# A four-stream graph-attention stack on one core: a clamp moved to ScalarE, new start times and pauses of the streams, and new transfer prices in its planner

## The chip, the core and the metric

The kernel runs on one core of a Trainium2 chip. The metric is device time in microseconds (us). The kernel before takes 2759.6 us, the median of 3 runs (2759.0 to 2762.83).

## The reference, cut to what matters

`x` is 32 batches of 512 nodes by 256 features, `adj` one 512 x 512 adjacency matrix for all. Each batch goes through four graph-attention layers, each one on the relu of a layer norm, with a residual:

```python
h = maximum(layernorm(x), 0); x = x + L0(h)      # attention, masked by adj, elu
h = maximum(layernorm(x), 0); x = x + L1(h)      # attention, masked by adj, relu
h = maximum(layernorm(x), 0); x = x + L2(h)      # the same with 4 heads of 64, elu
h = maximum(layernorm(x), 0); x = x + L3(h)
# L3: out = relu(x @ mlp1_w + b)                  (256 -> 512)
#     out = elu(_gat(out, no mask, W_fc)) + out   and _gat ends in an elu itself
#     out = relu(out @ mlp2_w + b)                (512 -> 256)
#     out = relu(elu(_gat(out, adj, W_hand)) + out)
```

So layer 3 holds two elus of an elu. With q = exp(v), the inner elu is max(v, 0) + min(q, 1) - 1, and the outer one on top adds exp(min(q, 1) - 1) - 1 on the negative side. All arithmetic is float32.

## The kernel before, in words

**Work.** A batch of 512 nodes is four tiles of 128 rows. A layer norms its rows (VectorE statistics at L653 and L654, ScalarE Ln and Exp for the root at L656 and L657, VectorE subtraction at L660 or L664), transposes them on TensorE (L442) and takes the relu on the way out of PSUM into `hT` (L674), multiplies by the weights (`values`, L434) into `v`, and builds the attention weights `w` (L737, one VectorE instruction for 128 x 512). For L737 a row of scores has to stand on all partitions: a short transpose, a copy on ScalarE (L749), a DMA of the row to DRAM (L751) and one that spreads it back over the 128 partitions (L757). The weighted sums run on TensorE (`averages`, L434), and VectorE takes the reciprocal of their denominator (L769). Layer 2 runs its four heads on quarters of the array (L438, "128*32"). Layer 3's unmasked attention is done by sorting in 31 of the 32 batches: rows are scattered to DRAM by an indirect DMA on GpSimd (L1025), prefix sums are made and written to a table (L1071), and the rows are gathered back (L1079). The last batch does it by plain sums (`attend`).

**The clamp.** `elu2_plus1` (L794 to L798) is called 194 times, 190 of them on 128 x 512: VectorE takes min(q, 1) (L796), ScalarE exp of that minus 1 (L797, the -1 is a bias column `minus1`), VectorE adds it to the relu part (L798).

**Four streams.** Batch b belongs to stream b mod 4; each stream is a Python generator that yields virtual times, and the loop over `ready` (L1190 to L1208) always runs the stream that is earliest. `after_us(u)` (L428) gives the virtual time of the next step: the step's begin, plus STRETCH times the TensorE time that it issued, plus SLOW times u. Stream i begins at i * LEAD + late. In its first batch a stream also waits PAUSES[3b + i] behind each of layers 0, 1 and 2. `setup`, which finishes the weights and the mask, is a fifth stream with its own spacing. All this only fixes the order in which the program is written.

**The planner.** The program is built twice. In the rehearsal `jobs_of` and `in_order` (L165 to L376) simulate it with a price for each instruction and let each engine take, of what is ready, what was written first; the order that results is then forced on each engine's queue (`arrange`). Two tiles of one buffer tag must open in the order in which they are written. So a stream that is written late can't open its first `xn` before the earlier-written streams have opened theirs, even where engines are idle. Transfers are priced in `price` (L110, its transfers from L126) by kind, from LANDING and SHORT; only loads of inputs also share a pipe of 350 bytes per ns (`job.flux`).

Of the kernel before, what the change touches and what calls it, by code (L numbers as in the profile page):

```python
# [67 lines left out]
class Job:  # L68
# [9 lines left out]
HANDOVER = {"PE": 40.0, "DVE": 33.0, "Activation": 33.0, "Pool": 70.0, "SP": 28.0}  # L78
LANDING = {
    "sums": 5600.0, "spread": 4300.0, "table": 6500.0, "x": 10000.0, "order": 4100.0, "g": 6800.0, "out": 4500.0,  # L80
    "adj": 9000.0,
}
SHORT = {"table": 5200.0, "row": 2600.0, "out": 4500.0}
SWITCH = 93.0
# [25 lines left out]
def price(job, outs, ins, in_psum):  # L110
# [15 lines left out]
    if op == "DMACopy":  # L126
        name, _, s = outs[0]
        kind = name.split("_")[0].rstrip("0123456789")
        large = elements(s) * s[0][1] > 5000
        job.took = LANDING.get(kind, 6000.0) if large else SHORT.get(kind, 3300.0)  # L130
        if kind == "spread":
            job.took += 900.0 * (ins[0][1] // 512)
        if ins[0][0].startswith("in_") and not (kind == "x" and ins[0][1] >= 4 * 512 * 256):
            job.took, job.flux = 2500.0, max(160.0, 4.0 * elements(s) * s[0][1] / 350.0)
        job.holds = (2000.0 if kind == "order" else 1290.0) if e == "Pool" else 600.0 if kind in ("sums", "table") else 400.0
        return
# [264 lines left out]
def fast(ctx, tc, plan, flag, x, adj, w0, a0, w1, a1, w2, a2, mlp1_w, mlp1_b, mlp2_w, mlp2_b,  # L401
# [9 lines left out]
    NS = 4  # L411
    LEAD = 81.69
    GO = 7.0
    PAUSES = (1.98, 20.79, 0, 9.87, 13.42, 5.98, 12.87, 2.43, 0, 28.8, 13.7, 0)
    SLOW = 1.53
    STRETCH = 1.75

# [35 lines left out]
    nc.vector.memset(eps, EPS)  # L453
    minus1 = const.tile([P, 1], FP, name="minus1")
    nc.vector.memset(minus1, -1.0)
    seen = const.tile([P, 5 * B], FP, name="seen")
# [219 lines left out]
    def turned(xn, when):  # L676

        hT = work.tile([P, KF, N], FP, tag="hT", name="hT", bufs=3)
        turn_pair(xn, hT, 0)
        yield when  # L680
        turn_pair(xn, hT, 2)
        yield after_us(0.26)
        return hT
# [8 lines left out]
    def values(hT, w, rs=None):  # L692

        v = work.tile([P, NT, F + 3], FP, tag="v", name="v", bufs=4)
        for t in range(NT):
            ps = bank()
            for k in range(KF):
                matmul(
                    ps[:, :F + 3], hT[:, k, t * P:(t + 1) * P], w[:, k, :], start=(k == 0), stop=(k == KF - 1)
                )  # L700
            pj = v[:, t, F:F + 1]
            if rs is None:
                nc.scalar.activation(v[:, t, F:], ps[:, F:F + 3], AF.Exp)
                nc.scalar.activation(v[:, t, :F], ps[:, :F], AF.Copy, scale=pj)
            else:
                nc.scalar.activation(v[:, t, F:], ps[:, F:F + 3], AF.Exp, scale=rs[:, t:t + 1])
                both = small([1], "both")
                nc.vector.tensor_tensor(both, rs[:, t:t + 1], pj, op=OP.mult)
                nc.scalar.activation(v[:, t, :F], ps[:, :F], AF.Copy, scale=both)
            if t + 1 < NT:  # L710
                yield after_us(0.32)
        yield after_us(0.7)
        return v

    def linear_t(inT, w, bias, name, bufs):
# [3 lines left out]
        for f in range(ft):  # L719
            p = bank()  # L720
            for k in range(kt):
                matmul(p, w[:, k, f * P:(f + 1) * P], inT[:, k, :], start=(k == 0), stop=(k == kt - 1))
            nc.scalar.activation(o[:, f, :], p, AF.Relu, bias=bias[:, f:f + 1])
            yield after_us(0.05 if f == ft - 1 else 2.73)
        return o
# [46 lines left out]
    def plain(hT, w, rs=None, far=False):  # L772
        v = yield from values(hT, w, rs)
        r = None
        if far:
            r = spread(rows_out(v[:, :, F + 2], 1)[0, :])
            yield after_us(11.34)
        wt = weights(lambda t: v[:, t, F + 2:F + 3], lambda j: v[:, j, F + 1:F + 2], r=r)
        note(v[:, :, F:])
        yield after_us(0.41)  # L780
        return v, wt
# [12 lines left out]
    def elu2_plus1(r, q):  # L794

        nc.vector.tensor_scalar(q, q, 1.0, None, op0=OP.min)  # L796
        nc.scalar.activation(q, q, AF.Exp, bias=minus1)  # L797
        nc.vector.tensor_tensor(r, q, r, op=OP.add)  # L798

    def layer0(xt, xn, rs, when):  # L800
        v, wt = yield from plain((yield from turned(xn, when)), W0, far=True)
        xn, rs = new_xn(), small([NT], "rs")
        for t0 in range(0, NT, 2):
            r, q = pair(), pair("q")
            for i in range(2):
# [3 lines left out]
                if i == 0:  # L809
                    yield after_us(0.56)  # L810
            add_elu(xt[:, t0:t0 + 2, :], r, q)
            norm(xt, xn, rs, t0, True)
            last, when = when, after_us(0.48)
            if t0 == 0:
                yield after_us(0)
        yield last
        return xn, rs, when

    def layer1(xt, xn, rs, when):
        v, wt = yield from plain((yield from turned(xn, when)), W1, rs, far=True)  # L820
        xn, rs = new_xn(), small([NT], "rs")
        for t0 in range(0, NT, 2):
            r = pair()
            for i in range(2):
                p, rd = averages(v, wt, t0 + i)
                nc.scalar.activation(r[:, i, :], p, AF.Relu, scale=rd)
                if i == 0:
                    yield after_us(3.06)
            xr = xt[:, t0:t0 + 2, :]
            nc.vector.tensor_tensor(xr, xr, r, op=OP.add)  # L830
            norm(xt, xn, rs, t0, True)
            last, when = when, after_us(1.98)
            if t0 == 0:
                yield after_us(0.04)
        yield last
        return xn, rs, when

    def layer2(xt, xn, rs, when):
        hT = yield from turned(xn, when)
        v = work.tile([P, NT, NH, CH], FP, tag="v", name="v2", bufs=4)  # L840
        for t in range(NT):
# [10 lines left out]
            )  # L852
            yield after_us(1.87 if t + 1 < NT else 0.3)
        row_d = rows_out(v[:, :, :, D + 2], NH)
# [3 lines left out]
        def begin():  # L858
# [3 lines left out]
            )  # L862
            return after_us(0.05)

# [5 lines left out]
        )  # L870
        yield after_us(14.86)
        begin()
        note(v.rearrange("p t h c -> p (t h) c")[:, :, D:])
        yield after_us(0.87)
        when = begin()
        for g, parts in enumerate(plan):
# [9 lines left out]
            nc.scalar.copy(s, p)  # L886
            yield after_us(1.08)
            if g < 2:
# [23 lines left out]
            if g:  # L912
# [3 lines left out]
                add_elu(xt[:, :, (g - 1) * 2 * D:g * 2 * D], y, q)  # L916
            yield after_us(3.1)
        xn, rs = new_xn(), small([NT], "rs")
        for t0 in range(0, NT, 2):
            norm(xt, xn, rs, t0, False)  # L920
        yield after_us(4.83)
        return xn, rs, after_us(1.14)

# [27 lines left out]
    def attend(oT, b):  # L951

        halves, ends = fc_values()
        for c in range(2):
            for t in range(NT):
                project_half(oT, halves, ends, c, t)
                yield after_us(0.48)
# [4 lines left out]
        yield after_us(0.73)  # L962
        ys = []
        for t in range(NT):
# [9 lines left out]
            ys.append(y)  # L974
            yield after_us(0.14)
            if t:
                mlp_in(oT, ys[t - 1], t - 1)
                yield after_us(0.1)
        yield after_us(0)
# [3 lines left out]
    def sort_attend(oT, b):  # L983
# [6 lines left out]
        for t in range(NT):  # L990
            project_half(oT, halves, ends, 0, t)
            yield after_us(1.43)
        project_half(oT, halves, ends, 1, 0)
        yield after_us(0.78)
# [3 lines left out]
        yield after_us(5.75)  # L998

# [8 lines left out]
        note(ends)  # L1008
        sort = after_us(3.88)
        yield after_us(0.32)  # L1010
        for t in range(1, NT):
            project_half(oT, halves, ends, 1, t)
            yield after_us(3.04)
        for t in range(NT):
# [6 lines left out]
        for c in range(2):  # L1021
# [17 lines left out]
            sort = after_us(0.46)  # L1039
        places = table[:N, :].rearrange("(p t) (k c n) -> p (t k) c n", t=NT, k=2, c=2)  # L1040
        sort = after_us(0.54)
        for c in range(2):
# [15 lines left out]
            yield after_us(1.92)  # L1058

# [12 lines left out]
            nc.sync.dma_start(table[N:, c * C:(c + 1) * C], tot[P - 1:, :])  # L1072
            sort = after_us(6.33)
        yield after_us(12.5)
        got, when, gs = [], [], []
# [10 lines left out]
        gather(1)  # L1086
        landed = after_us(9.82)
        for t in range(NT):
# [12 lines left out]
            got.append(y)  # L1101
            landed = after_us(0.46)
            when.append(after_us(12.63))
            if t == 0:
# [4 lines left out]
        mlp_in(oT, got[-1], NT - 1)  # L1109
        yield after_us(0.11)  # L1110

    def layer3(xt, xn, when, b):
# [6 lines left out]
        for t0 in range(0, NT, n):  # L1119
            y, q = pair()[:, :n, :], pair("q")[:, :n, :]  # L1120
            for i in range(n):
                p, rd = averages(v, wt, t0 + i)
                nc.scalar.activation(q[:, i, :], p, AF.Exp, scale=rd)
                nc.scalar.activation(y[:, i, :], p, AF.Relu, scale=rd)
                yield after_us(0)
            elu2_plus1(y, q)
# [39 lines left out]
    def batch(b):  # L1166
        if b < NS:
            first_norm(b)
            yield after_us(20.8)
        else:  # L1170
            yield after_us(0.8)
        xt, xn, rs = normed.pop(b)
        when = after_us(2.46)
        for i, layer in enumerate((layer0, layer1, layer2)):
            xn, rs, when = yield from layer(xt, xn, rs, when)
            if b < NS:
                yield after_us(PAUSES[3 * b + i])
        if b + NS < B:
            xts[b + NS] = load_x(b + NS)
# [9 lines left out]

    ready = {i: i * LEAD + late for i, late in enumerate((0, 4.35, 4.97, 5.59))}  # L1190
    streams = [stream(i) for i in range(NS)]
    early = setup()
    ready[NS] = 1.42
    while ready:
        i = min(ready, key=ready.get)
        if i == NS:
            turn[0] = NS - 1
            ready[i] += 19.61
            if next(early, early) is early:
# [463 lines left out]
```

## Time and profile before

| what | value |
|---|---|
| median of 3 runs | 2759.6 us |
| the profiled execution, its own time | 2780.08 us |
| its span, first to last instruction | 2778.3 us |
| granted TensorE clock, mean | 0.993 |
| PE busy | 2711.2 us, 98% |
| DVE (VectorE) busy | 2288.7 us, 82% |
| ACT (ScalarE) busy | 1625.7 us, 59% |
| POOL (GpSimd) busy | 515.4 us, 19% |
| chain that ended last | PE 69%, DVE 23%, ACT 5% |

Times in the profile are of one execution. Busy times of PE are modelled where matmuls overlap, so that an instruction's duration on PE is longer than the distance to the next. A wait is written as "who <- what it waited for"; idle time of an engine that isn't the bound costs nothing. Groups are told apart by line, engine, tile names and shape.

### The profile page before, as it was taken

The page shows a single profiled execution, that of the slowest core. Times are in us where ns is not written, and L with a number is a line of the kernel's source. Part 1 is how long each engine was busy: PE and PEld are TensorE (multiplying, and loading weights), DVE is VectorE, ACT ScalarE, POOL GpSimd, SP SyncE. Part 2 cuts the span into 40 slices and gives each one's busy share as a digit, 9 for nine tenths or more (in the row PEclk, how much of TensorE's full clock was granted, in tenths as well). Part 3 has the DMA queues.
Part 4 walks back from the last instruction along what each step waited for, and adds up shares of the span by engine and source line. Part 5 has one row for each costly group of instructions (what it writes and reads, how often), then busy time and mean ns, then how long its engine had stood idle before and what let it go on. Part 6 is the DMA issues. An engine that isn't in the chain of part 4 may idle for free.

```text
span 2778.3 us, 41413 instructions
## 1 busy us (share of the span) xinstructions
PE 2711.2 (98%) x13944; PEld 1906.2 (69%) x13944; DVE 2288.7 (82%) x5889; ACT 1625.7 (59%) x4228; POOL 515.4 (19%) x516
## 2 busy tenths in 40 slices
PE   5999999999999999999999999999999999999998
PEld 4666677766767676676767667676676766777655
DVE  5788888888878889788897888978989789888875
ACT  3455666566556565555765566655665556565554
POOL 0012221212112221012221222111221112212120
PEclk8999999999999999999999999999999999999999
DMA  4033333334424343144341434423443234333331
GB/s 129 24 103 113 125 122 103 122 107 134 137 77 133 122 132 123 60 136 138 126 134 60 126 131 133 131 69 113 147 136 109 89 115 138 126 102 114 116 131 37
DMA packets 214885, 314.04 MB, mean 113 GB/s; under 512 B 17356, under 2 KB 156934, under 8 KB 214664
## 3 DMA queue, kind: packets, MB, share of 16 engines
q1 hardware_dynamic: 184904, 213.01, 24.8%
q0 software_dynamic: 29760, 98.30, 10.3%
q8 instruction: 112, 1.84, 0.3%
q14 instruction: 109, 0.89, 0.1%
HBM read 195.61 MB, written 115.65 MB: 112 GB/s over the span
## 4 chain that ended last, share of the span: by engine, by line
PE 69%; DVE 23%; ACT 5%; issue 1%; DMA 1%; SPq 0%; another core or an unknown queue 0%; DVEq 0%
PE b L434 54%; PE b L438 8%; PE b L442 7%; DVE w L737 6%; DVE st L653 2%; DVE sums L1055 1%; DVE y L798 1%; DVE xn L664 1%; DVE sums L1070 1%; DVE xn L660 1%; DVE y L1134 1%; ACT q L797 1%; DVE sums L1063 1%; DVE y L791 1%; DVE g L1093 1%
## 5 line engine op out<-in xcount | busy, mean ns | idle before, releaser
L434 PE MATMUL b<-v,w 128*128 128x257 f32 (+1 forms) x3136 | 756.5, 382 | 16.8 <-DVE w L737 14.8
L434 PEld LDWEIGHTS b<-v,w 128*128 128x128 f32 x3136 | 576.8, 190 | 141.9 <-issue 30.6
L737 DVE SCALAR_TENSOR_TENSOR w<-spread,v,maskT 128x512 f32<-128x512 f32 x896 | 651.7, 760 | 26.1 <-DMA spread<-row 26.1
L434 PE MATMUL b<-WFC,oT 128*128 128x256 f32 (+1 forms) x2048 | 504.7, 381 | 0.0
L434 PEld LDWEIGHTS b<-WFC,oT 128*128 128x128 f32 x2048 | 373.2, 189 | 79.3 <-issue 26.1
L434 PE MATMUL b<-W,hT 128*128 128x259 f32 (+1 forms) x1536 | 387.2, 388 | 0.8 <-ACT hT L674 0.8
L1025 POOL DMA_INDIRECT order<-v,at x248 | 264.1, 1065 | 628.3 <-DVE w L737 194.7
L438 PE MATMUL b<-w,v 128*32 128x512 f32 x3072 | 349.5, 595 | 0.0
L434 PEld LDWEIGHTS b<-W,hT 128*128 128x128 f32 x1536 | 277.5, 192 | 56.5 <-issue 12.0
L1079 POOL DMA_INDIRECT g<-table,at x124 | 137.9, 1112 | 889.4 <-DMA table<-sums 194.8
L434 PE MATMUL b<-hT,WM 128*128 128x512 f32 x512 | 239.8, 593 | 1.2 <-ACT hT L674 1.2
L434 PE MATMUL b<-oT,WM 128*128 128x512 f32 x512 | 234.8, 603 | 4.7 <-DVE oT L1152 4.7
L438 PEld LDWEIGHTS b<-w,v 128*32 128x32 f32 x3072 | 89.9, 109 | 196.4 <-issue 196.0
L653 DVE BATCH_NORM_STATS2 st<-x 128x6 f32<-128x256 f32 x512 | 193.3, 408 | 5.5 <-DMA x<-in_x_dram 3.4
L798 DVE TENSOR_TENSOR y<-q,y 128x512 f32<-128x512 f32 (+1 forms) x194 | 135.7, 700 | 57.3 <-ACT q L797 48.8
L442 PE MATMUL b<-ident,xn 128*128 128x128 f32 x1024 | 163.4, 280 | 17.9 <-DVE xn L660 6.8
L442 PEld LDWEIGHTS b<-ident,xn 128*128 128x128 f32 x1024 | 121.7, 141 | 72.0 <-DVE xn L664 15.3
L434 PEld LDWEIGHTS b<-oT,WM 128*128 128x128 f32 x512 | 98.4, 193 | 105.5 <-issue 96.7
L674 ACT ACTIVATE hT<-b 128x512 f32<-128x512 f32 x256 | 150.5, 592 | 26.1 <-PE b L442 25.1
L949 ACT ACTIVATE v<-b,ends 128x256 f32<-128x256 f32 x256 | 119.6, 471 | 66.6 <-PE b L434 62.4
L769 DVE RECIPROCAL rden<-b 128x1 f32<-128x1 f32 x388 | 59.2, 161 | 118.9 <-PE b L434 116.0
L1137 POOL TENSOR_TENSOR x<-x,y 128x512 f32<-128x512 f32 x62 | 86.3, 1392 | 368.9 <-ACT y L1135 365.0
(145 smaller groups left out, 4028.0 us busy)
## 6 DMA issues: line engine op xcount, KB each, us to landing
spread<-row SPq DMA_DIRECT2D x255, 256.0 KB
table<-sums SPq DMA_DIRECT2D x62, 1032.0 KB
sums<-order SPq DMA_DIRECT2D x62, 516.0 KB
x<-in_x_dram SPq DMA_DIRECT2D x32, 512.0 KB
out_dram<-x SPq DMA_DIRECT2D x62, 256.0 KB
sums<-order SPq DMA_DIRECT2D x62, 129.0 KB
order<-v,at POOLq DMA_INDIRECT x248
row<-row SPq DMA_DIRECT2D x127, 2.0 KB
```

Source lines behind the costliest of these rows:

```text
L434: nc.tensor.matmul(p, w, x, **flags)
L438: nc.tensor.matmul(p, w, x, tile_position=(0, c), **flags)
L442: nc.tensor.transpose(p, x, i)
L653: nc.vector.bn_stats(st[:, i, :], xt[:, t0 + i, :])
L674: nc.scalar.activation(hT[:, :, t0 * P:(t0 + 2) * P], p.rearrange("p (k n) -> p k n", k=KF), AF.Relu)
L737: nc.vector.scalar_tensor_tensor(wt[:, j, :], r, t_col(j), maskT[:, j, :], op0=OP.max, op1=OP.mult)
L769: nc.vector.reciprocal(r, den)
L798: nc.vector.tensor_tensor(r, q, r, op=OP.add)
L949: nc.scalar.activation(halves[c][:, t, :F], ps[:, :F], AF.Copy, scale=ends[:, t, 0:1])
L1025: one = nc.gpsimd.indirect_dma_start(out=orders[c], out_offset=bass.IndirectOffsetOnAxis(ap=at[:, 0, t:t + 1], axis=0), in_=halves[c][:, t ...
L1079: nc.gpsimd.indirect_dma_start(out=g, out_offset=None, in_=table, in_offset=bass.IndirectOffsetOnAxis(ap=at[:, 1, t:t + 1], axis=0),)
L1137: (nc.gpsimd if n == 2 else nc.vector).tensor_tensor(xr, xr, y, op=OP.add)
```

## The change

Three things change. The clamp of `elu2_plus1` goes to ScalarE: relu(1 - q), then exp of minus that, which is exp(min(q, 1) - 1). The streams begin at other virtual times, their pauses in the first batch are others, and the second half of the turn of a first batch's next layer counts from behind the pause. The planner prices every transfer as a latency by kind plus its bytes over one common pipe of 300 bytes per ns. Some 45 constants in `after_us(...)` all over the layers are others too; the diff shows those of the set-up and of the batch, and a few of the rest.

```diff
-LANDING = {
-    "sums": 5600.0, "spread": 4300.0, "table": 6500.0, "x": 10000.0, "order": 4100.0, "g": 6800.0, "out": 4500.0,
-    "adj": 9000.0,
-}
-SHORT = {"table": 5200.0, "row": 2600.0, "out": 4500.0}
+LANDING = {"sums": 2800.0, "spread": 2800.0, "table": 3000.0, "x": 6000.0, "order": 3300.0, "g": 3900.0, "out": 1900.0, "row": 2300.0}
+RATE = 300.0
...
-        large = elements(s) * s[0][1] > 5000
-        job.took = LANDING.get(kind, 6000.0) if large else SHORT.get(kind, 3300.0)
-        if kind == "spread":
-            job.took += 900.0 * (ins[0][1] // 512)
+        job.flux = (132096.0 if kind == "order" else 4.0 * elements(s) * s[0][1]) / RATE
+        job.took = LANDING.get(kind, 2500.0)
         if ins[0][0].startswith("in_") and not (kind == "x" and ins[0][1] >= 4 * 512 * 256):
-            job.took, job.flux = 2500.0, max(160.0, 4.0 * elements(s) * s[0][1] / 350.0)
+            job.took = 2500.0
+            job.flux = max(160.0, 0.86 * job.flux)
...
-    LEAD = 81.69
+    LEAD = 84.68
     GO = 7.0
-    PAUSES = (1.98, 20.79, 0, 9.87, 13.42, 5.98, 12.87, 2.43, 0, 28.8, 13.7, 0)
-    SLOW = 1.53
-    STRETCH = 1.75
+    PAUSES = (4.86, 2.65, 0.3, 5.68, 42.54, 1.59, 27.54, 15.47, 13.82, 37.26, 84.31, 26.93)
+    SLOW = 1.65
+    STRETCH = 1.83
...
-    minus1 = const.tile([P, 1], FP, name="minus1")
-    nc.vector.memset(minus1, -1.0)
+    plus1 = const.tile([P, 1], FP, name="plus1")
+    nc.vector.memset(plus1, 1.0)
...
     def elu2_plus1(r, q):
 
-        nc.vector.tensor_scalar(q, q, 1.0, None, op0=OP.min)
-        nc.scalar.activation(q, q, AF.Exp, bias=minus1)
+        nc.scalar.activation(q, q, AF.Relu, bias=plus1, scale=-1.0)
+        nc.scalar.activation(q, q, AF.Exp, scale=-1.0)
         nc.vector.tensor_tensor(r, q, r, op=OP.add)
...
-        sort = after_us(0.54)
+        sort = after_us(17.89)
...
-            when.append(after_us(12.63))
+            landed = after_us(1.3)
+            when.append(after_us(0.14))
...
         if b < NS:
             first_norm(b)
-            yield after_us(20.8)
+            yield after_us(1.8)
         else:
-            yield after_us(0.8)
+            yield after_us(2.83)
         xt, xn, rs = normed.pop(b)
-        when = after_us(2.46)
+        when = after_us(2.49)
         for i, layer in enumerate((layer0, layer1, layer2)):
             xn, rs, when = yield from layer(xt, xn, rs, when)
             if b < NS:
                 yield after_us(PAUSES[3 * b + i])
+                when = after_us(3.08)
...
-    ready = {i: i * LEAD + late for i, late in enumerate((0, 4.35, 4.97, 5.59))}
+    ready = {i: i * LEAD + late for i, late in enumerate((0, -67.04, -73.49, -221.51))}
...
-    ready[NS] = 1.42
+    ready[NS] = 3.36
...
-            ready[i] += 19.61
+            ready[i] += 2.04
```

More of the change, by code (lines that the diff above doesn't have):

```diff
@@ L681, in turned @@
         turn_pair(xn, hT, 2)
-        yield after_us(0.26)
+        yield after_us(1.8)
         return hT
@@ L710, in values @@
             if t + 1 < NT:
-                yield after_us(0.32)
-        yield after_us(0.7)
+                yield after_us(0)
+        yield after_us(0)
         return v
@@ L723, in linear_t @@
             nc.scalar.activation(o[:, f, :], p, AF.Relu, bias=bias[:, f:f + 1])
-            yield after_us(0.05 if f == ft - 1 else 2.73)
+            yield after_us(0.64 if f == ft - 1 else 1.18)
         return o
@@ L776, in plain @@
             r = spread(rows_out(v[:, :, F + 2], 1)[0, :])
-            yield after_us(11.34)
+            yield after_us(9.9)
         wt = weights(lambda t: v[:, t, F + 2:F + 3], lambda j: v[:, j, F + 1:F + 2], r=r)
         note(v[:, :, F:])
-        yield after_us(0.41)
+        yield after_us(2.61)
         return v, wt
@@ L809, in layer0 @@
                 if i == 0:
-                    yield after_us(0.56)
+                    yield after_us(1.61)
             add_elu(xt[:, t0:t0 + 2, :], r, q)
             norm(xt, xn, rs, t0, True)
-            last, when = when, after_us(0.48)
+            last, when = when, after_us(1.58)
             if t0 == 0:
-                yield after_us(0)
+                yield after_us(2.48)
         yield last
@@ L827, in layer1 @@
                 if i == 0:
-                    yield after_us(3.06)
+                    yield after_us(0.12)
             xr = xt[:, t0:t0 + 2, :]
@@ L831, in layer1 @@
             norm(xt, xn, rs, t0, True)
-            last, when = when, after_us(1.98)
+            last, when = when, after_us(0.95)
             if t0 == 0:
-                yield after_us(0.04)
+                yield after_us(1.99)
         yield last
@@ L852, in layer2 @@
             )
-            yield after_us(1.87 if t + 1 < NT else 0.3)
+            yield after_us(0.64 if t + 1 < NT else 0.43)
         row_d = rows_out(v[:, :, :, D + 2], NH)
@@ L862, in begin @@
             )
-            return after_us(0.05)
+            return after_us(0.35)
         Q = D // 2
@@ L870, in layer2 @@
         )
-        yield after_us(14.86)
+        yield after_us(10.51)
         begin()
         note(v.rearrange("p t h c -> p (t h) c")[:, :, D:])
-        yield after_us(0.87)
+        yield after_us(0.2)
         when = begin()
@@ L886, in layer2 @@
             nc.scalar.copy(s, p)
-            yield after_us(1.08)
+            yield after_us(2.88)
             if g < 2:
@@ L916, in layer2 @@
                 add_elu(xt[:, :, (g - 1) * 2 * D:g * 2 * D], y, q)
-            yield after_us(3.1)
+            yield after_us(0.65)
         xn, rs = new_xn(), small([NT], "rs")
@@ L920, in layer2 @@
             norm(xt, xn, rs, t0, False)
-        yield after_us(4.83)
-        return xn, rs, after_us(1.14)
+        yield after_us(7.93)
+        return xn, rs, after_us(1.01)
     def fc_values():
@@ L956, in attend @@
                 project_half(oT, halves, ends, c, t)
-                yield after_us(0.48)
+                yield after_us(0.8)
             if c == 0:
@@ L961, in attend @@
         wt = weights(lambda t: ends[:, t, 2:3], lambda j: ends[:, j, 1:2], masked=False)
-        yield after_us(0.73)
+        yield after_us(0.26)
         ys = []
@@ L974, in attend @@
             ys.append(y)
-            yield after_us(0.14)
+            yield after_us(0.7)
             if t:
                 mlp_in(oT, ys[t - 1], t - 1)
-                yield after_us(0.1)
+                yield after_us(0.15)
         yield after_us(0)
@@ L991, in sort_attend @@
             project_half(oT, halves, ends, 0, t)
-            yield after_us(1.43)
+            yield after_us(0)
         project_half(oT, halves, ends, 1, 0)
-        yield after_us(0.78)
+        yield after_us(0.56)
         for c in range(2):
@@ L997, in sort_attend @@
         tj = spread(rows_out(ends[:, :, 1], 1)[0, :])
-        yield after_us(5.75)
+        yield after_us(7.55)
         found = small([2, NT], "found")
@@ L1008, in sort_attend @@
         note(ends)
-        sort = after_us(3.88)
-        yield after_us(0.32)
+        sort = after_us(6.87)
+        yield after_us(3.82)
         for t in range(1, NT):
             project_half(oT, halves, ends, 1, t)
-            yield after_us(3.04)
+            yield after_us(1.04)
         for t in range(NT):
@@ L1038, in sort_attend @@
                     tc.add_manual_dep(read.ins, other.ins.name, landed, reason="rows of four tiles")
-            sort = after_us(0.46)
+            sort = after_us(1.18)
         places = table[:N, :].rearrange("(p t) (k c n) -> p (t k) c n", t=NT, k=2, c=2)
-        sort = after_us(0.54)
+        sort = after_us(17.89)
         for c in range(2):
@@ L1057, in sort_attend @@
                 )
-            yield after_us(1.92)
+            yield after_us(3.28)
             pv = bank()
@@ L1072, in sort_attend @@
             nc.sync.dma_start(table[N:, c * C:(c + 1) * C], tot[P - 1:, :])
-            sort = after_us(6.33)
-        yield after_us(12.5)
+            sort = after_us(0.51)
+        yield after_us(10.38)
         got, when, gs = [], [], []
@@ L1086, in sort_attend @@
         gather(1)
-        landed = after_us(9.82)
+        landed = after_us(8.63)
         for t in range(NT):
@@ L1101, in sort_attend @@
             got.append(y)
-            landed = after_us(0.46)
-            when.append(after_us(12.63))
+            landed = after_us(1.3)
+            when.append(after_us(0.14))
             if t == 0:
@@ L1109, in sort_attend @@
         mlp_in(oT, got[-1], NT - 1)
-        yield after_us(0.11)
+        yield after_us(1.95)
     def layer3(xt, xn, when, b):
@@ L1124, in layer3 @@
                 nc.scalar.activation(y[:, i, :], p, AF.Relu, scale=rd)
-                yield after_us(0)
+                yield after_us(0.4)
             elu2_plus1(y, q)
@@ L1168, in batch @@
             first_norm(b)
-            yield after_us(20.8)
+            yield after_us(1.8)
         else:
-            yield after_us(0.8)
+            yield after_us(2.83)
         xt, xn, rs = normed.pop(b)
-        when = after_us(2.46)
+        when = after_us(2.49)
         for i, layer in enumerate((layer0, layer1, layer2)):
```

## The prediction, made before the change was run

> **What bounds the kernel now.** I began with the page's first part, busy time by engine, then took the same by stages, to see whether the share is an average over unlike parts. The columns are the stretch, its length, then busy time and instructions of PE, PEld (weight loads), DVE, ACT and POOL, the granted clock, the DMA engines' share and GB/s.
>
> ```profile
> PE 2711.2 (98%) x13944; PEld 1906.2 (69%) x13944; DVE 2288.7 (82%) x5889; ACT 1625.7 (59%) x4228; POOL 515.4 (19%) x516
> ```
>
> ```profile
> 0.00:40.00 40.00, 18.23 (x69) 14.86 (x70) 17.43 (x59) 9.38 (x24) 1.69 (x10) 0.83 0.67 210
> 40.00:120.00 80.00, 68.05 (x359) 48.81 (x358) 63.70 (x205) 35.12 (x104) 3.88 (x9) 0.96 0.08 27
> 120.00:260.00 140.00, 133.76 (x692) 88.81 (x691) 104.99 (x281) 75.94 (x201) 22.29 (x24) 0.99 0.29 91
> ```
>
> ```profile
> 794.00:1130.00 336.00, 334.88 (x1736) 235.39 (x1735) 285.67 (x729) 202.85 (x528) 65.48 (x64) 1.00 0.37 117
> ```
>
> The last row is one round of four batches in the middle of the run; the chain of the work that ended last repeats itself every 335 to 336 us. There PE is busy for 334.88 of 336 us. In the first 120 us it is busy for 86.
>
> A busy PE isn't a PE at its peak, so I counted its stream too. Ends of neighbouring matmuls of one shape stand 217 ns apart for 257 columns, 216 to 226 for 256 to 268, 429 for 512, 109 for a transpose, and 107.5 for one of layer 2's quarter-array matmuls. Times the counts in the groups by line and shape (3104 x 0.217 + 3072 x 0.1075 + 1024 x 0.653 for the three shapes of 256 to 259 columns + 512 x 1.303 for the four groups of 512 + some 2360 transposes x 0.109 + 36 for the rest) that makes some 2630 us. The span is 148 us longer: 62 are lost in the first 336 us, 8 to 10 in each of the next six rounds, 16 in the one after them, 15 in the last 93 us. Of a round's 9, some 7.6 are the 12 changes into and out of layer 2's quarter tiles (0.44 and 0.20 us more than the pitch), which the change leaves. **So a middle round has 1.3 us to give, seven of them 9 us. What there is to gain lies at the start.**
>
> PE's waits in the first 120 us, and the timeline round the longest, show why the start is thin:
>
> ```profile
> PE b L434 <- DVE w L737: 13.1, 2, 12.1
> PE b L442 <- DMA W<-in_L_gnn_W_dram: 5.8, 1, 5.8
> PE b L442 <- DVE xn L660: 4.4, 2, 3.7
> PE b L442 <- ACT rs L656: 3.5, 1, 3.5
> ```
>
> ```profile
> 22.31 0.24 ACT L749 COPY row<-b 4x128 f32<-4x128 f32 x1
> ...
> 26.93 0.43 SPq L751 DMA_DIRECT2D row<-row  x1
> 30.47 0.35 SPq L757 DMA_DIRECT2D spread<-row  x1
> 33.55 2.08 DVE L737 SCALAR_TENSOR_TENSOR w<-spread,v,maskT 128x512 f32<-128x512 f32 x3 [7.21 <-DMA spread<-row]
> 34.35 5.68 PEld L434 LDWEIGHTS b<-v,w 128*128 128x128 f32 x17 [12.31 <-DVE w L737]
> 34.35 5.87 PE L434 MATMUL b<-v,w 128*128 128x257 f32 x16 [12.12 <-DVE w L737]
> ```
>
> Batch 0 is alone: its row is copied at 22.3, SP issues it at 26.9, behind loads of the set-up, and until its spread has landed at 33.5 DVE idles 7.2 us and PE 12.1. Batch 1, whose x was issued at 3.4 and, at the 294 GB/s of the first 20 us, is there by about 10, takes no part: its first transposes run at 54.0, because it is written 86 virtual us later.
>
> **The clamp.** Three groups of the view by line and shape price it (count, then busy us and mean ns, then the idle time before them): L796 goes, L797 loses its bias column, and a relu with a bias column comes.
>
> ```profile
> L796 DVE TENSOR_SCALAR q<-q 128x512 f32<-128x512 f32 x190 | 84.0, 442 | 39.0 <-ACT q L1096 23.9 <-ACT q L1123 12.3 <-ACT q L971 2.5
> ```
>
> ```profile
> L797 ACT ACTIVATE q<-q,minus 128x512 f32<-128x512 f32 x190 | 135.8, 715 | 24.9 <-DVE q L796 23.7
> ...
> L1135 ACT ACTIVATE y<-y 128x512 f32<-128x512 f32 x62 | 39.0, 629 | 35.7 <-DVE y L1134 33.8 <-DVE rden L769 1.6
> ```
>
> DVE loses 84.0 + 1.9 (four on 256 columns) = 86 us: 2288.7 becomes 2203. ACT gains 190 x 0.715 + 4 x 0.503 = 138 for the relu (as L797, with a column) and loses 190 x (0.715 - 0.629) = 16: 1625.7 becomes 1747, 63%. In a middle round that is DVE 286 to 275 and ACT 203 to 218 of 336: neither is a bound, before or after.
>
> The latency of a pair changes otherwise. Today DVE's min (0.44) runs beside ACT's relu of the other half (0.71), so the second exp comes right behind that relu. Afterwards ACT does relu, relu, exp in a row: 0.715 + 0.629 - 0.715 = 0.63 us later. PE's waits for the sum at L798 are 4.1 us, four times, all behind 2640 us; if each gets 0.63 longer, that is +2.5 us. Were every pair on the path, it would be 190 x 0.63 = +120; below nothing, DVE's 86 us could free at most the 9 us that the middle rounds have. I take **+1**: half of the four cases, and one microsecond won back in the rounds.
>
> On this the Trainium skill speaks against the change: "ScalarE: Activation LUTs", in its rules for kernel authors, wants relu, max and min on VectorE, as faster per element. The rows agree on the price, 442 against 715 ns, and by the rule alone the sum would be 0.27 x 194 = 53 us worse; but on the rows ACT has 133 us of a round free, so I count none of it.
>
> **The prices of transfers** cost no instruction; they move orders. A spread was priced 4.3 us and is now 2.8 + 262144/300 = 3.67. Where DVE waited for one, it began 3.0 to 3.5 us behind the issue (30.47 to 33.55 above). A table goes from 6.5 to 3.0 + 3.44 = 6.44; GpSimd's waits show 6.1 to 6.3. A gather goes from 6.8 to 5.66; DVE's waits show 5.0 to 7.4. So the new prices stand nearer to the trace, and the spread's still lies above it, which adds no wait. One flaw speaks the other way: the pipe is a queue in order of issue, latency included, so a spread behind an 8-us load of x is planned some 5 us late. Bounds for the rounds: at best the 9 us, at worst one spread a round planned amiss by the 3 us between a gather's old and real landing, 7 x 3 = +20. I take **0**, as the middle rounds lie against PE's own stream.
>
> **The starts.** Virtual starts go from 0, 86, 168, 251 to 0, 17.6, 95.9, 32.5, and the set-up's pieces are written within 20 virtual us rather than 190. Streams 1 and 3 can now put their first halves into the 12.1-us hole: a first norm takes DVE 4 x (0.408 + 0.168 + 0.444) = 4.1 us, the turn and values take PE 8 x 0.109 + 16 x 0.219 = 4.4. DVE's idle 7.2 us there holds most of two norms, PE's 12.1 two times 4.4 = 8.8. I take 8.8 us won. From 40 to 120 us the stream falls 19 us short (7.3, 3.3, 6.4 and 2.1 in four stretches of 20), with DVE idle for 16; other streams' work can fill what DVE is able to feed: half, 9.5. The following 140 us I leave. Sum of the start: **-18**, between 0 and -31 (12.1 + 19).
>
> SP has more to do early: each stream's row and spread are queued behind the loads there, as the 4.4 us from copy to issue show; this is why I don't take the whole hole.
>
> **The end.** The same order of streams drains; streams now lie 87 to 90 virtual us apart rather than 61 to 124. The last 138 us lose 27, of which about 13 lie in the last 20 us, a chain that stays. -5 to +5; I take **-2**.
>
> Sum: -18 + 1 + 0 - 2 = -19 us. The profiled execution took 2780.08 us by itself, its span 2778.3; the sum gives a span of 2759. The median without the profiler is 2759.6, 0.7% lower, and with the same 19 us the forecast is **2741 us** (-0.7%).
>
> **Rivals.** *Crowding at the start, slower.* Layers 0 to 2 of one batch need DVE for 10.5 + 9.7 + 23.5 = 43.7 us (layer 2: 16 x 0.760 for w, 4 x 0.480 for v, 2 x 1.37 for the elus, 4 x 1.02 for the norms, 2.7 for the rest) and PE for 11.4 + 11.4 + 18.1 = 40.9. If four streams go through them abreast, DVE has 4 x (43.7 + 4.1) + 24 for the set-up = 215 us to do while PE has 164: PE idles for 51, and for some 18 more until DVE has its first data. Before, the first 336 us lost 62 - 8 for tile changes = 54. So +15: 2775 us. It decides if layer 3, which is PE's (84 less 41 us of PE a batch; of DVE 71 less 48 = 23), begins in no stream before the others reach layer 2. For it: DVE is at 80% from 40 to 120 already. Against it: the long pauses, 42.5 behind stream 1's and 84.3 behind stream 3's layer 1, times 1.65. *Given back, no change:* the hole fills, but PE waits for the same spreads later, since SP issues them one behind the other; 2759 to 2760 us. *The whole hole and more:* -31 at the start, -9 in the rounds, -4 at the end: 2716 us. *The order doesn't change at the start:* if buffers (three `xn`, four `w`) hold the streams apart anyway, only the clamp remains, +1: 2761.
>
> **How the numbers follow.** The forecast's case, -6 to -35 us, has 0.60; the whole hole 0.06; no change, by giving back or by buffers, 0.10; crowding or a worse order in the rounds 0.24. About 0.2%, 5.5 us, is what a measurement of this kernel can tell from no change. So faster 0.66, same 0.10, slower 0.24. The range reaches to the two outer cases with their unknowns, 2716 to 2778 (crowding plus the clamp's 2.5): outside lie some 0.04 below and 0.12 above. The likeliest case's own range is 2725 to 2754.
>
> **What would show it.** Right: the wait for L737 near 34 us is under 6 us; batch 1's transposes run before 34 us; PE is busy for more than 100 of the first 120 us; DVE stands near 2203, ACT near 1747; a middle round still takes 335 to 336. Wrong: PE's waits between 40 and 260 us are on L737 or on norms and longer than before (crowding); a middle round over 337 us (the planner's new order, not the start, decides); waits for L798 in the rounds (the clamp is on the path).

## The result

The changed kernel takes 2752.84 us (2749.64 to 2754.95, 11 runs), the kernel before on the same chip 2760.84 us (11 runs): a ratio of 0.9967, interval 0.9959 to 0.9974, or -8 us. It is faster, as forecast, by less than half of the 19 us forecast, and 2741 is 12 us too low. Beside before on two chips taken later the ratio was again 0.9962 (0.9948 to 0.9977) and 0.9967 (0.9955 to 0.998); on one more ("the fourth chip" below), where before took 2781.7 us, it was 1.0050 (1.0034 to 1.0067).

The profiled executions are 28 us apart (spans 2778.3 and 2750.3), the medians 8: the first profile of before caught an execution 19 us above the median of its kernel. Two later ones have spans of 2767.3 and 2765.6 us.

The profile after, busy time by engine and by the stages shown of before (same columns):

```profile
PE 2698.7 (98%) x13944; PEld 1913.4 (70%) x13944; DVE 2221.8 (81%) x5695; ACT 1725.1 (63%) x4422; POOL 516.2 (19%) x516
```

```profile
0.00:40.00 40.00, 27.03 (x117) 21.54 (x118) 31.13 (x122) 17.95 (x52) 4.72 (x17) 0.91 0.69 217
40.00:120.00 80.00, 77.10 (x431) 58.66 (x430) 66.30 (x207) 41.73 (x126) 1.45 (x3) 1.00 0.10 31
120.00:260.00 140.00, 134.86 (x709) 84.25 (x707) 106.21 (x264) 70.37 (x175) 22.55 (x24) 0.98 0.31 98
796.00:1132.00 336.00, 335.22 (x1756) 237.76 (x1749) 276.75 (x704) 215.72 (x553) 66.44 (x64) 1.00 0.37 118
```

PE is busy for 104 of the first 120 us, before for 86; DVE works 31 of the first 40 us rather than 17. In a middle round DVE has gone from 286 to 277 and ACT from 203 to 216; over the whole run DVE stands at 2222 and ACT at 1725 us, where 2203 and 1747 were expected. PE's waits in the first 120 us, and the timeline at the place of the former hole:

```profile
PE b L438 <- DVE xn L660: 6.0, 4, 3.5
PE b L438 <- DMA W<-in_L_gnn_W_dram: 5.8, 1, 5.8
PE b L430 <- DVE w L733: 2.6, 2, 1.4
```

```profile
23.95 0.69 PE L438 MATMUL b<-ident,xn 128*128 128x128 f32 x2 [3.46 <-DVE xn L660]
24.85 0.32 SPq L747 DMA_DIRECT2D row<-row  x1
...
26.35 1.07 PE L430 MATMUL b<-W,hT 128*128 128x259 f32 x2
...
27.64 3.84 PE L430 MATMUL b<-W,hT 128*128 128x259 f32 x14
...
28.15 0.35 SPq L753 DMA_DIRECT2D spread<-row  x1
```

L733 is before's L737. Its wait of 12.1 us is gone: while batch 0's row goes out at 24.85 and its spread at 28.15, PE multiplies another batch's `hT` (L430, 16 matmuls). The clamp's lines (L792 has taken the place of L796):

```profile
L792 ACT ACTIVATE q<-q,plus 128x512 f32<-128x512 f32 x190 | 135.6, 714 | 0.3
L793 ACT ACTIVATE q<-q 128x512 f32<-128x512 f32 x190 | 118.7, 625 | 1.1
```

**Where the time went.** PE's stream, counted as in the prediction, is 2630 us in every run, so what a run loses is its span less 2630. The table has the lost time by how much of the stream is done; "300 to 2500" are the rounds. The first two rows were taken on one chip, and their difference, 9.1 us, stands for the result.

| kernel (span) | to 175 us | 175 to 300 | 300 to 2500 | 2500 to 2625 | the rest |
|---|---|---|---|---|---|
| before, third profile (2765.6) | 52.5 | 2.7 | 56.0 | 14.0 | 10.3 |
| after, fourth profile (2756.5) | 30.0 | 15.3 | 51.9 | 19.8 | 9.4 |
| before, second profile (2767.3) | 55.6 | 2.6 | 53.7 | 14.6 | 10.7 |
| after, third profile (2752.3) | 30.1 | 14.9 | 47.4 | 20.4 | 9.4 |

Up to 175 us of stream the change wins 22.5 us. By 300 it has given 12.6 back; the rounds win 4.1, the stretch to 2625 loses 5.8, the rest wins 0.9.

### The profile page after: what moved, and what is told of

Its sections match the earlier page's. It is cut to its first block, busy times and chain, and to the rows that moved or that the text cites. A ratio compares the mean times of both kernels' runs of the same rounds, so it can differ in the third digit from the quotient of the medians.

```text
span 2750.3 us, 41381 instructions
## 1 busy us (share of the span) xinstructions
PE 2698.7 (98%) x13944; PEld 1913.4 (70%) x13944; DVE 2221.8 (81%) x5695; ACT 1725.1 (63%) x4422; POOL 516.2 (19%) x516
## 3 DMA queue, kind: packets, MB, share of 16 engines
q0 software_dynamic: 29760, 98.30, 10.5%
## 4 chain that ended last, share of the span: by engine, by line
PE 73%; DVE 19%; ACT 4%; DMA 2%; issue 1%; POOL 0%; SPq 0%; DVEq 0%; ACTq 0%
PE b L430 57%; PE b L434 9%; PE b L438 7%; DVE w L733 7%; DMA spread<-row 1%; DVE st L649 1%; DVE sums L1059 1%; DVE y L787 1%; DVE sums L1066 1%; DVE x L788 1%; DVE sums L1051 1%; DVE y L794 1%; ACT q L792 1%; ACT q L793 1%; ACT q L1092 1%
## 5 line engine op out<-in xcount | busy, mean ns | idle before, releaser
L430 PE MATMUL b<-v,w 128*128 128x257 f32 (+1 forms) x3136 | 758.1, 381 | 8.5 <-DVE w L733 4.6
L733 DVE SCALAR_TENSOR_TENSOR w<-spread,v,maskT 128x512 f32<-128x512 f32 x896 | 650.9, 768 | 45.3 <-DMA spread<-row 40.2
L430 PEld LDWEIGHTS b<-v,w 128*128 128x128 f32 x3136 | 573.7, 190 | 123.1 <-issue 24.1
L430 PE MATMUL b<-WFC,oT 128*128 128x256 f32 (+1 forms) x2048 | 496.7, 381 | 0.0
L430 PEld LDWEIGHTS b<-WFC,oT 128*128 128x128 f32 x2048 | 376.8, 189 | 76.1 <-issue 15.9
L430 PE MATMUL b<-W,hT 128*128 128x259 f32 (+1 forms) x1536 | 378.4, 386 | 0.2 <-ACT hT L670 0.2
L430 PEld LDWEIGHTS b<-W,hT 128*128 128x128 f32 x1536 | 283.0, 191 | 66.5 <-issue 19.1
L430 PE MATMUL b<-hT,WM 128*128 128x512 f32 x512 | 239.2, 594 | 1.1 <-ACT hT L670 1.1
L430 PE MATMUL b<-oT,WM 128*128 128x512 f32 x512 | 229.3, 601 | 3.6 <-DVE oT L1148 3.6
L794 DVE TENSOR_TENSOR y<-q,y 128x512 f32<-128x512 f32 (+1 forms) x194 | 132.2, 681 | 85.5 <-ACT q L793 84.9
L430 PEld LDWEIGHTS b<-oT,WM 128*128 128x128 f32 x512 | 98.1, 193 | 115.8 <-issue 108.0
L438 PE MATMUL b<-ident,y 128*128 128x128 f32 x896 | 135.1, 276 | 13.4 <-DVE y L794 12.0
```

The lines of the kernel that those rows point to most:

```text
L430: nc.tensor.matmul(p, w, x, **flags)
L438: nc.tensor.transpose(p, x, i)
L733: nc.vector.scalar_tensor_tensor(wt[:, j, :], r, t_col(j), maskT[:, j, :], op0=OP.max, op1=OP.mult)
```

## The experiments

**The same two kernels again.** No edit; four profiles on other chips.

> The kernel before, unchanged, profiled a second time. The first profile of before took 2780 us beside a median of 2761, that of after 2752 beside a median of 2753, so the two profiles stand 28 us apart where the medians stand 8 apart. Theory A: 20 us of the first profile are an accident of that execution, mostly in the start, where GpSimd, SP and the loads have no fixed times; then this profile's span is 2755 to 2762 and PE's wait of 12 us for L737 near 34 us is shorter by much. Theory B: the profiler lengthens before, and not after, since before stands on waits for transfers and after does not; then the span is again 2774 to 2782, with the hole of 12 us and rounds of 335.8 us, and the ratio of the unprofiled runs is 1.000 with an interval of some 0.001.

Ratio 1.0006 (0.9996 to 1.0015). The profiled execution is 1.4 us above the median of its run, where the first profile stood 19 us above: that one was an accident, as in theory A, and the profiler does not lengthen before, against theory B. But PE waits 13.8 us for L737, so the hole belongs to before, against the rest of theory A. Against this profile the first one lost 5 us more between 175 and 300 us of stream and 6 to 7 more in the rounds.

> The changed kernel, unchanged, profiled a second time beside the kernel before. If the result stands on the order alone and not on the chip, the ratio is again 0.9960 to 0.9975. By the profiles so far, of the stream's lost time after has 44 us in its first 300 us of stream against 58 to 62 before, 47 in the rounds against 54 to 60, and 20 behind 2500 us of stream against 15; theory A expects this profile to repeat 42 to 46, 44 to 50 and 19 to 22, so that start and end are fixed parts, -15 and +6, and the rounds are worth the rest.

The ratio is 1.0050, the other way. Start and end repeat (46.2 lost to 300 us, 19.4 at the end), the rounds lose 100 us rather than 47.

> The changed kernel a third time, beside the kernel before on the same chip, as the base of the next three. On two chips so far it stood at 0.9967 and at 1.005 of before; on the second the transfers landed later (a table 6.4 to 8.6 us behind its issue, on the first 5.9 to 7.5). Theory S: after's order leaves less slack behind transfers, so its ratio to before follows their landing; between 0.995 and 1.007, near 1.005 if tables land behind 6.4 us or more again. Rival: the chip's speed makes both slower alike, and the ratio was an accident: 0.996 to 0.998.

The ratio is 0.9962, so of the chips measured the fourth is the exception.

> The kernel before, profiled a third time, on the chip of the next run. Expected: ratio 1.000; lost time of TensorE's stream 56 to 62 us in the first 300 us of stream, 44 to 54 from 300 to 2500, 14 to 16 from 2500 to 2625.

> The changed kernel, profiled a fourth time, on the same chip as the third profile of before. Expected: 0.995 to 0.998 of before; lost 43 to 46 us in the first 300 us of stream, 46 to 49 from 300 to 2500, 20 to 21 from 2500 to 2625: so against before on the same chip -13 to -16 at the start, -5 to +3 in the rounds, +5 to +6 at the end.

The ratios are 0.9992, which is no change, and 0.9967; the table's first two rows are these profiles. Their difference is -9.9 us at the start rather than -13 to -16, and +5.8 at the end. In the rounds both lose more than expected, 56.0 and 51.9.

**One part alone, planned anew.** Into before: the starts, pauses, set-up spacing and steps of the batch (e3), or the prices (e4). In after, put back: the clamp (e6), those starts (e7), the prices (e8). The edits are the parts of the diff above.

> Before with the new stream starts, pauses, spacing of the set-up and steps of the batch alone; clamp, prices and the constants in the layers as before. Theory A (the start's hole is not in a usual execution): -3 to -8 us. The prediction's term: -18 us, from the hole near 34 us and the 80 us behind it. Rival: the constants inside the layers were tuned together with the starts, so that the rounds get a worse order: +5 to +30 us in the rounds, with the first 336 us still shorter by 15 or more.

> Before with the new prices of transfers alone. The prediction's term: 0 us, between -9 and +20. If the better prices are worth something of themselves, rounds fall from 335.8 towards after's 333.3 us, -2 x 7 = -14 us; if the queue of the pipe misplaces transfers behind loads of x, DVE's waits for L737 grow and rounds pass 337, +10 or more.

> The changed kernel with the clamp back on VectorE, and planned anew with it. Theory T (every constant of a kernel is tuned to all the others, so that a part put back costs, whichever way it goes): +20 to +80 us over after. Rival C (the clamp on ScalarE is a cost of 55 us that the new order only hides): faster than after by up to 10 us. Rival D (the clamp carries the gain through DVE's 86 us): +5 to +15, rounds 335 rather than 333.5.

> The changed kernel with the old starts, pauses, set-up spacing and steps of the batch. The prediction's term for the starts: +18 us, all of it in the first 300 us of stream (lost there: 58 to 62 rather than 44), the rounds as in after. Theory T: the rounds are worse too, since the phases of the streams in all rounds follow from the starts: +20 to +90, most of it behind the first 300 us of stream.

> The changed kernel with the old prices of transfers. The prediction's term: 0. Theory T: +20 to +80, spread over the rounds. If the new prices are worth something by being nearer to the chip, it loses more here than the old prices gained when the new ones were put into before (73 us slower).

| kernel | ratio to before | lost to 175 | 175 to 300 | 300 to 2500 |
|---|---|---|---|---|
| before with new starts | 1.0307 (1.0290 to 1.0325) | 35.6 | 22.6 | 138 |
| before with new prices | 1.0269 (1.0252 to 1.0286) | 60.0 | 7.7 | 106 |
| after with old clamp | 1.0294 (1.0269 to 1.0319) | 30.7 | 15.0 | 156 |
| after with old starts | 1.1073 (1.1051 to 1.1094) | 78.5 | 25.3 | 316 |
| after with old prices | 1.0434 (1.0407 to 1.0461) | 34.0 | 34.4 | 176 |

The last three ran on the fourth chip, where after itself is at 1.0050. Every part by itself costs 2 to 10%, whichever way it goes, nearly all in the rounds. That is theory T, and beyond its own price for the old starts and the old prices, which cost 286 and 111 us over after. None of these mixtures fits together, so a part planned anew says little of the part. One thing can be read all the same: the gain to 175 us of stream comes with the starts, for before with new starts has 35.6 there, after with the old starts 78.5. What is given back by 300 us can't be put down to them: it is 22.6 in before with new starts, but 25.3 in after with the old ones too.

**The clamp alone, in a kept order.** To part the instructions from the plan, these kernels rehearse the original and force its order on every engine; only the clamp is moved.

```diff
     def elu2_plus1(r, q):
-        nc.vector.tensor_scalar(q, q, 1.0, None, op0=OP.min)
-        nc.scalar.activation(q, q, AF.Exp, bias=minus1)
+        if plan:
+            nc.scalar.activation(q, q, AF.Relu, bias=plus1, scale=-1.0)
+            nc.scalar.activation(q, q, AF.Exp, scale=-1.0)
+        else:
+            moved.append(nc.vector.tensor_scalar(q, q, 1.0, None, op0=OP.min).ins.name)
+            nc.scalar.activation(q, q, AF.Exp, bias=plus1)
...
+            order["DVE"].remove(places[name])
+            line.insert(line.index(places[name] + 1), places[name])
```

> Before with the clamp alone on ScalarE; the order on all engines is that which the planner made for the VectorE clamp, with each relu put straight ahead of its exp in ScalarE's line. So this is the instructions' own worth, without a new order. Prediction's term: +1 us, with DVE at 2203 and ACT at 1747 busy, DVE's idle time larger by 86, rounds unchanged. Rival: ScalarE's line is longer by 15 us a round and evictions from PSUM come later, so that PE waits for banks: +10 to +20 us. Other rival: DVE was what PE's last losses stood on, so -8 us, which would be the whole result.

The ratio is 1.0202 (1.0185 to 1.0219), +55 us: the rival, at three times its price. PE's waits between 500 and 2600 us of this run:

```profile
PE b L442 <- DVE y L803: 10.4, 13, 1.2
PE b L434 <- ACT hT L675: 6.2, 6, 1.0
PE b L442 <- ACT rs L657: 5.3, 6, 0.9
PE b L442 <- ACT y L891: 5.2, 6, 0.9
PE b L442 <- ACT v L710: 3.5, 6, 0.7
PE b L434 <- ACT y L831: 2.6, 6, 0.4
```

The longest in sum is the wait for the clamp's own sum (L803, before's L798). Besides, PE stands once a round before each of five ScalarE lines, evictions of PSUM and roots of the norms. In the second profile of before, on the same chip, the same stretch has 3.8 us of waits in all, 0.4 of them for the sum and 0.5 for one of these five lines.

The second such kernel puts the relu where its input is ready by the plan, rather than ahead of its exp (`job.at = max(other.done for other in job.real)`, and the line sorted by it).

> Before with its order kept and the clamp on ScalarE, now at the place in ScalarE's line where its input is ready by the plan, not straight ahead of its exp. If the 55 us of the first such kernel came from the place, this loses under 15 us or gains up to 9; if ScalarE's line is simply 0.63 us longer at each pair, ahead of evictions that TensorE waits for, it loses 35 to 70 again, with TensorE's waits on ScalarE's lines (hT, rs, v) as in that run.

The ratio is 1.0171 (1.0154 to 1.0188), +49 us, and 99 us are lost in the rounds. PE's longest waits in the same stretch:

```profile
PE b L447 <- DVE y L808: 15.2, 27, 1.0
PE b L439 <- ACT hT L680: 7.2, 6, 1.2
PE b L447 <- ACT rs L662: 5.4, 6, 0.9
PE b L447 <- ACT y L896: 5.2, 6, 0.9
```

So the place of the relu is not the cause. What both runs share is the relu on ScalarE: the sum (L808 here) comes later, and so does what is queued on ScalarE. Which of the two weighs more is not parted.

The reverse, in after's order, with the VectorE clamp where its input is ready:

> After, with its order kept, and the clamp back on VectorE at the place in VectorE's line where its input is ready by the plan. The instructions' own worth in after's order. By before's counterpart (55 us lost to the ScalarE clamp) either way of moving it off the plan costs: +20 to +60 over after. If the ScalarE clamp is by itself a loss that the new order only bears, this is faster than after by 5 us or more; if DVE's 86 us are by themselves the gain, it is slower by 5 to 20.

2762.75 us, ratio to before 1.0002 (0.9992 to 1.0011), beside 2753.95 for after on the same chip: 8.8 us slower. **After without its clamp on ScalarE is no faster than before.** Its rounds lose 57.5 rather than 47.4, its end 17.9 rather than 20.4. A middle round takes 335.0 us, the mean of five; in after it takes 333.3 (333.9 in the fourth profile), in the second and third profile of before 334.8 and 335.2. To see whether that is VectorE's time or the way through VectorE, the last of these keeps ScalarE's clamp and adds a useless instruction in its place on VectorE:

```diff
+        if plan:
+            fillers.append(nc.vector.tensor_reduce(spare, WM1[:, 0, :F], AX.X, OP.max).ins.name)
         relu = nc.scalar.activation(q, q, AF.Relu, bias=plus1, scale=-1.0)
```

> After, with its order and its ScalarE clamp kept, and an instruction of no use on VectorE (a maximum over 128 x 256, some 0.42 us, 194 times) at the places where the VectorE clamp stood in the run before. It puts VectorE's time back without the way of the data through VectorE. Theory V (VectorE's time is what the clamp's move saves): +7 to +11 us over after, like the VectorE clamp's 9. Theory W (the two handovers between engines and the wait in VectorE's line are what it saves): 0 to +3.

The time is 2771.75 us beside 2758.61 for after on the same chip: +13 us, 12 of them in the rounds. This is theory V, a little above its price: VectorE's time alone is enough to cost what the move saved. The 194 fillers took 79 us of VectorE, the clamp 83; why they cost 13 us and the clamp 8.8 isn't shown (with the fillers ScalarE keeps its relu and is busy for 1722 us, with the clamp for 1636). PE's waits between 500 and 2600 us of that run name what came late:

```profile
PE b L447 <- ACT y L897: 3.5, 6, 0.7
PE b L439 <- DVE w L745: 3.3, 6, 0.5
PE b L447 <- DVE xn L668: 3.1, 6, 0.6
```

In the fourth profile of after, on the same chip, the same stretch has 1.7 us on the first of these lines, 1.0 on `w` and nothing on this norm.

**Slack behind transfers.** Before and after with their orders kept and a second write of each table to a spare one:

```diff
+            if plan:
+                spare = spares[b % 2][:N, :].rearrange("(p t) (k c n) -> p (t k) c n", t=NT, k=2, c=2)
+                extra.append(nc.sync.dma_start(spare[:, :, c, :], flat[c]).ins.name)
             nc.sync.dma_start(places[:, :, c, :], flat[c])
```

> Before, with its order kept, and a second write of the same 1 MB to a spare table ahead of each table write; this makes tables land later, by up to 3.5 us at the 300 GB/s that loads reached, 62 times. Theory S: before has a planned step of 12.5 us and more between table and gather, and behind a gather another 19 us to its transposes, so it loses little: 0 to +15 us. Rival: both orders lose alike, +30 or more.

> After, with its order kept, and the same second write of each table. Theory S: after has 0.2 us of planned time between a gathered tile and its transposes, and GpSimd waits for the table 13 times already; it loses +40 to +150 us over after, at least three times what before loses. Rival: as before's loss, within 20 us.

The ratios are 1.0502 (1.0481 to 1.0523) and 1.0319 (1.0302 to 1.0337): before loses 140 us, after 97. Tables did land later: where GpSimd waited for one, it began 8.9 to 10.5 us behind the issue, in the first profiles, without the second write, 5.9 to 7.9. Theory S fell: after's order is the less tender of the two to this load. Why after loses to before on the fourth chip stays open.

**The stretch where the start's gain is given back.** In the first profile of after PE runs dry at 220.9 us:

```profile
220.25 0.60 PE L430 MATMUL b<-WFC,oT 128*128 128x256 f32 x2
224.88 1.11 PE L438 MATMUL b<-ident,y 128*128 128x128 f32 x4 [4.02 <-DVE y L794]
225.78 1.06 PE L438 MATMUL b<-ident,xn 128*128 128x128 f32 x4
```

```profile
222.60 0.61 ACT L793 ACTIVATE q<-q 128x512 f32<-128x512 f32 x1
...
223.77 0.39 DVE L649 BATCH_NORM_STATS2 st<-x 128x6 f32<-128x256 f32 x1
224.08 0.16 DVE L650 BATCH_NORM_AGGREGATE mv<-st 128x2 f32<-128x6 f32 x1
...
224.16 0.66 DVE L794 TENSOR_TENSOR y<-q,y 128x512 f32<-128x512 f32 x1
```

```profile
218.00:224.80 6.80, 2.85 (x14) 2.08 (x12) 6.00 (x20) 6.51 (x14) 4.22 (x4) 0.90 0.35 123
224.80:229.00 4.20, 3.87 (x17) 3.07 (x17) 2.81 (x8) 4.14 (x13) 3.20 (x4) 0.50 0.78 256
```

PE waits 4.02 us for the sum behind the clamp of the first gathered tile (L794), and behind the wait the granted clock is 0.50: four transposes take 1.11 us, which took 0.60 at full clock. This agrees with the Trainium skill, "TensorE: Matmul & The Clock Gate", part 1, where an idle window of some 3.4 us halves the clock. Round the hole (218 to 224.8 us) the engines that feed PE are nearly full, ACT with 6.51 and DVE with 6.00 of 6.80 us, and the sum stands in DVE's line: its exp (L793) is done at 223.2, and it starts at 224.16, behind a norm's statistics.

Two runs halved a pause of a stream behind its layer 1 (stream 3: 84.31 to 42.15; stream 1: 42.54 to 21.27).

> After with stream 3's pause behind layer 1 at 42.15 rather than 84.31, planned anew. If pauses starve TensorE, stream 3's layer 2 stands ready in the hole near 222 us: lost between 175 and 300 us of stream falls from 15 to 5 or less. If the gather is the cause, it stays at 12 or more. The rounds follow from the phases of the streams and may be worse by 20 to 300 us, as in the runs with other starts; this doesn't bear on the question.

> After with stream 1's pause behind layer 1 at 21.27 rather than 42.54, planned anew. The same two outcomes for the stretch from 175 to 300 us of stream: 5 or less if the pauses starve TensorE, 12 or more if the first gather does. Rounds may be worse as above.

Neither outcome: from 175 to 300 us of stream they lose 51 and 46 us, and in all 1.1125 (1.1093 to 1.1157) and 1.1031 (1.0985 to 1.1077) of before. The first does lose only 2.0 us between 175 and 200 us of stream, where the fourth profile of after loses 9.0, but the holes come back behind it. Whether the pauses, the first gather or the full lines of ACT and DVE starve PE there can't be told from them.

## Why the prediction was wrong

- **PE bounds the rounds: right. What they have to give: wrong.** A round takes 334.8 to 335.8 us before, 333.3 to 333.9 after. The floor was the mis-sized term. The first of a group of four quarter-array matmuls ends 0.55 us behind the matmul ahead of it, and its other three almost together with it: the fourth ends at 0.566 us, where a group of four otherwise takes 0.430. So a change into the quarter tiles costs 0.13 us and not 0.44, which set the first of four against the mean pitch of one. With 0.20 for the change out, the twelve pairs make some 4 us a round rather than 7.6, and a middle round had some 5 us to give, not 1.3.
- **The hole and the 80 us behind it, -18: right in kind, and more than that.** To 175 us of stream it is -22.5 (30.0 against 52.5). PE was busy for 104 of the first 120 us, where over 100 was asked; L733 waits 1.4 us at most.
- **"The following 140 us I leave": the step that failed first.** This stretch was put at nothing without a reason. From 175 to 300 us of stream, at 205 to 345 us of the run, 12.6 us are given back, more than half of the gain, so that the start is worth -9.9 and not -18. The prediction had read the pauses as the remedy against crowding, and did not ask what PE has to do while streams stand in them. The wait is not the one that the rival of crowding named, L737 or a norm; it is the sum behind the clamp of the first gathered tile, 4.0 us in the first profile and 4.6 in the fourth. But crowding at that place isn't excluded, with ACT and DVE as full there as the rows show. That the second half of the gain is spent again is near the rival "given back", but through a hole at the first gather, not through spreads one behind the other.
- **The end, -2: wrong, +5.8 to 2625 us of stream and +4.9 to the last instruction.** 2.5 of it is the clamp (20.4 less 17.9 in the kept order), as much as the four waits of 0.63 us that were counted; PE's waits for the sum there are now six, 6.4 us in all, and were four, 4.1 us. The rest comes with the order.
- **The clamp, +1: wrong in sign in this order.** It is -8.8 us by medians. The step that failed is "DVE's 86 us could free at most the 9 us that the middle rounds have", kept as the far end and weighed at one: 10 us were won in the rounds, and the 9 stood on the floor that was too high. The other side was too light as well: "ACT has 133 us of a round free" does not say that ScalarE has room ahead of the sum or of an eviction, and in before's order the same instructions cost 49 to 55 us. The rule of the Trainium skill that was weighed, "ScalarE: Activation LUTs", rules for kernel authors, to have relu, max and min on VectorE, holds for the instruction (442 against 714 ns) and for before's order, and not for after's.
- **Busy times, 2203 and 1747: both changes too large.** DVE fell by 67 us, not 86, and ACT rose by 99, not 122. The prediction added durations of instructions; the rows of neighbours on one engine overlap (on DVE they add up to 2681 us in before, of which 2289 are busy).
- **Prices, 0:** not to be told alone. Planned anew the new ones cost 72 us in before and the old ones 111 in after.
- **The sum.** By medians in after's order, starts, prices and constants together give -0.5 us (1.0002), where -20 was expected (-18 for the start, 0 for the prices, -2 for the end), and the clamp -8.8, where +1 was. The order wins its 10 us in the first 300 us of stream with either clamp, and its rounds are as long as before's (335.0 us); some 3 of the 10 are lost at the end, and where the others went is open, since before was not profiled on that chip. These two shares hold for this one way from before to after. Taken the other way round, the clamp costs 49 to 55 us in before's order, and the new plan then wins 58 to 63. So the right direction was luck: two errors of opposite sign. On the fourth chip the direction fails too, 2795 us beside 2782.

## What to carry to other kernels

Ask of an order fixed by a planner for the instructions and for the plan apart: keep the order by force and move one instruction, since any part planned anew moved this kernel by 2 to 11%. What an instruction is worth then holds for that order: the same move cost 49 to 55 us in one and won 8.8 in the other. A gain in a start-up has to be followed until the steady state begins, because it can be spent again there, as 12.6 of 22.5 us were here. And a mean busy share, 59% here, tells nothing of the room ahead of the one eviction that the busiest engine waits for.

## What the runs showed of the hardware

The same program stood at 0.9962 to 0.9967 of before in three measurements and at 1.0050 on a fourth chip, where the loss lay in the rounds. Late tables don't explain it: where GpSimd waited for a table, it began 6.4 to 8.6 us behind the issue there, on the chip of the first two rows of the table 6.3 to 9.3 in all waits but one, with 7.6 us as the middle value on both, and the rounds lost 100 us on the one and 51.9 on the other. In the rounds of the fourth chip PE also waits 8.5 us for nothing that the profile shows ("issue"), which it does in no other profile of after; the cause is open. The kernel before took 2761 to 2782 us over the chips, a spread larger than what this change is worth.
